# A preactivation chain of four convolution layers on one core: where the U-Net's 5x5 layer, conv2 and conv3 put their outputs

## The chip, the cores and the metric

The kernel runs on one core of a Trainium2 chip. The metric is the device time of one execution in microseconds (us). A core has engines that run side by side, each with its own instruction queue: TensorE (PE, matrix products into PSUM), VectorE (DVE) and ScalarE (ACT, both elementwise), GpSimd (POOL, here only the issue of some table loads) and SyncE (SP, here the issue of nearly all DMA transfers). [...]

## The reference

The input x has 16 samples, 32 channels, 128 x 128 pixels, float32. Four layers follow each other, each with a normalisation in front and a residual sum: a diagonal LSTM (layer 0), an adder layer (layer 1), a layer in the Hartley domain (layer 2) and an edge U-Net (layer 3). Cut to what matters here, layer 3 is:

```python
# five edge operators, each normalised over its sample: 32 -> 160 channels
b = [norm(corr3x3(x, op)) for op in (SOBEL, SCHARR, LAPLACE, ROBERTS, PREWITT)]
y = conv3x3(concat(b), conv1)          # 160 -> 32 channels, 128 x 128
y = maxpool2(y)                         # 64 x 64
y = maxpool2(conv3x3(y, conv2))         # 32 x 32
y = maxpool2(conv3x3(y, conv3))         # 16 x 16
y = conv3x3(y, conv4)                   # 16 x 16
y = conv3x3(deconv2x2(y, deconv1), conv5)   # 32 x 32
y = conv3x3(deconv2x2(y, deconv2), conv6)   # 64 x 64
y = conv3x3(deconv2x2(y, deconv3), conv7)   # 128 x 128
```

Layer 1 is `out[n,f] = -sum |patch - w|` over the 288 values of a 3x3 patch, on quantised values.

## The kernel before

**Stages.** `stage0` does layer 0. Then the samples are taken in four groups of four (`g`, 0 to 3), and 128 partitions hold 4 samples x 32 channels (`blk` is the sample, 32 partitions each). The adder layer (`Differences`) is computed sample by sample and half by half: 72 taps per half (8 blocks of channels x 9), each one instruction of 8192 or 8320 float16 values on ScalarE (L757) or VectorE (L760), summed over channels by TensorE (L647). Layers 2 and 3 (`After`) of a group can begin when its four samples have left the adder layer.

**The order of the work.** A planner, `Weave`, puts the work of `After` for groups 0 to 2 between the taps while the program is built. It keeps planned times of TensorE, VectorE and ScalarE (`weave.pe`, `weave.dve`, `weave.act`), to which the code adds an estimate of each step; each tap goes to the engine that is planned to end it first. `weave.later(us, step)` puts a step off to a planned time, `weave.done(v)` emits it at once, and `yield` hands TensorE time or a pause back to the planner. In this part (the front) `keep_order` fixes the order on every engine as emitted. When the taps are over, `drain` emits the rest of group 2 and the whole of group 3 (`end`, with more buffers) alternately by their planned times; there, the order on the engines is set by the framework's scheduler.

**The first layer of the U-Net.** The five operators and conv1 are one 5x5 convolution, whose weights depend on statistics of the sample: `statistics` (L1401) makes Gram products (L1428) of the frame, VectorE turns them into scales (`es_*`), and `first_layers` folds five tables `v`, loaded through POOL's queue, into the weights `wf` (L1559, L1561). The frame of a group lies in buffers `xp`, a ring of 2 in groups 0 to 2 and of 4 in group 3, each with 20 padded rows of 132 values: a chunk `ch` is 16 rows with two more on each side. `frames` loads the chunks (`load`), normalises them on ScalarE (L1373), stores them padded in DRAM (`store`, `xn`) and, for `conv1`, reads them again from there (`again`, two transfers a chunk).

`conv1` computes chunk by chunk, eight in all. TensorE works in 32 x 32 tiles: for each of 25 taps there are 16 matmuls, one for each sample `blk` and each of four groups of output partitions `j` (L1747). Bank `acc[blk]` then holds sample `blk`; its partitions `32j..` hold the rows 4j to 4j+3 of the chunk, all channels. Before the chunks, `conv1` computes corrections for the left and right border (L1721) into the tile `cut`. Per chunk and bank, VectorE adds two of them to the border columns (L1782), pools 2x2 (`pooled`, L1674) into a 128 x 128 tile, and `spread` adds the bias and writes `y1`. In `y1`, `y2`, `y3` and `y4` the partitions are again sample and channel, `[128, n+2, n+2]` with a border of zeros (`padded`), so the four groups of 32 partitions of a bank go to the same 32 partitions of the target: `spread` takes one instruction for each `j`, four a bank, sixteen a round, on ScalarE for the 5x5 layer and VectorE for conv2 to conv4 (L1685, L1688); in the last phase, when group 3 is alone (`weave.alone`), by halves on both.

```python
for j in range(4):
    d, s = dst(slice(32 * blk, 32 * blk + 32), j), src[32 * j : 32 * j + 32]
```

The emission of a chunk's `spread` is put off by 5 us (`weave.later(5.0, spread)`). That of the last chunk, `rest_of_y1`, is emitted before the second half of conv2.

**The small layers.** `small_layers` runs conv2 (two rounds of 4 x 8 rows), conv3 (one round of 4 x 8 rows), conv4 (one round of 4 x 4), each with 9 taps of 16 matmuls a round (L1597), then the two upsampling layers (L905, L930). `last` does the third upsampling, the residual sum (L1876, L1846) and the output.

Of the kernel before, what the change touches and what calls it, by code (L numbers as in the profile page):

```python
# [492 lines left out]
def rest(nc, tc, cst, sel16, bias, m1, r1, a, d, out):  # L493


    with ExitStack() as ctx:
# [16 lines left out]
        end.buffers = {"t_x": 8, "xm": 8, "xw": 4, "t_w": 6, "t_r": 8, "frames": 4, "gm": 5, "e_v": 6, "l_x": 4}  # L513
# [445 lines left out]
class After:  # L959
# [386 lines left out]
    def frames(self, g, pool):  # L1346
# [5 lines left out]
        ring = [pool.tile([128, 20, W + 4], F32, name=f"xp{i}") for i in range(self.buffers["frames"])]  # L1352
# [4 lines left out]
        chunk = lambda ch: ring[ch % len(ring)]  # L1357

# [35 lines left out]
        def again(ch, half):  # L1394

            own = slice(10 * half, 10 * half + 10)
            nc.sync.dma_start(chunk(ch)[:, own, :], padded(ch, own.start, own.stop))

        return load, normalise, store, again, chunk

    def statistics(self, g, pool, frames, sides, out, tables):  # L1401
# [8 lines left out]
        load, normalise, store, again, chunk = frames  # L1410
# [26 lines left out]
        for ch in range(H // 16):  # L1437
# [3 lines left out]
            for l in range(2, 18):  # L1441
# [29 lines left out]
                def following(ch=ch, half=half):  # L1471
                    if ch + ahead < H // 16:
                        load(ch + ahead, half)
                        ready[ch + ahead, half] = normalise(ch + ahead, half, 18.0)
                    else:
                        again(ch + ahead - H // 16, half)
# [56 lines left out]
    def first_layers(self, g, fp, frames, y2):  # L1533
# [32 lines left out]
        with self.pool("e_y1") as y1p:  # L1566
            y1 = self.padded(y1p, 64, "y1")
# [5 lines left out]
    def small_layers(self, cp, rp, y1, y2):  # L1573
# [3 lines left out]
        if not y1:  # L1577
# [3 lines left out]
            y3, y4, y5 = (self.padded(cp, n, f"y{i}") for n, i in ((16, 3), (16, 4), (32, 5)))  # L1581
# [3 lines left out]
        def conv(src, n, name, evict):  # L1585
            rows = min(n // 4, 512 // n)
            for r in range(0, n, 4 * rows):
                acc = [self.acc() for _ in range(4)]
                if r:
                    weave.done(self.rest_of_y1)  # L1590
                for tap in range(9):
                    kh, kw = tap // 3, tap % 3
                    for j in range(4):
                        for blk in range(4):
                            part = slice(32 * blk, 32 * blk + 32)
                            at = r + rows * j + kh
                            nc.tensor.matmul(  # L1597
                                acc[blk][32 * j : 32 * j + 32, : rows * n],
                                wc[name][part, tap, :],
                                src[part, at : at + rows, kw : kw + n],  # L1600
                                start=tap == 0,
                                stop=tap == 8,
                            )
                    yield rows * n / 512 * 1.0 + 0.15
                yield SUMMED
                for blk in range(4):
                    evict(r, rows, acc[blk][:, : rows * n], blk)
                yield -2.0

        def pool_into(dst, n, b):  # L1610
            def evict(r, rows, acc, blk):
                top, half = 1 + r // 2, rows // 2
                self.spread(
                    lambda part, j: dst[part, top + half * j : top + half * j + half, 1 : 1 + n // 2],
                    self.pooled(cp, acc, rows, n),
                    blk,
                    bias[:, b : b + 1],
                    nc.vector,
                )

            return evict

        def flat(r, rows, acc, blk):
            self.spread(
                lambda part, j: y4[part, 1 + r + rows * j : 1 + r + rows * j + rows, 1:17],
# [65 lines left out]
    def conv1(self, g, pool, frames, y1, sides, wf, b1):  # L1691
# [45 lines left out]
        for ch in range(H // R):  # L1737
# [37 lines left out]
            if ch + ahead < H // R:  # L1775
                for half in range(2):
                    again(ch + ahead, half)
# [277 lines left out]
```

## Time and profile before

| what | time |
|---|---|
| median of three runs | 6687.31 us (6674.74 to 6688.99) |
| the profiled execution | 6656.74 us |
| its span, first to last instruction | 6655.0 us |
| layer 0 | to about 685 us |
| first to last tap of the adder layer | 685.5 to 5586.6 us |
| the rest of groups 2 and 3 | to 6655.0 us |

The profile shows one execution. Its page gives busy time by engine, the span in 40 slices, the chain that ended last, and groups of instructions by source line, with the number of instructions, their busy time, the mean of one in ns, and the idle time of the engine just before them with what ended it. `32x128 f32` is partitions by elements. Other views answer by stretches of time, by tile, or instruction by instruction. `issue` is time in which an engine waited for nothing that the profile shows. TensorE takes a float32 matmul as two records.

### The profile page before, as it was taken

The numbers are of one execution on the slowest core, as the hardware profiler recorded it, in microseconds if no ns is written. First come the engines' busy times: TensorE is split into PE (matmuls) and PEld (weight loads), VectorE is DVE, ScalarE is ACT, GpSimd is POOL, SyncE is SP. The second block draws the span as 40 slices with busy tenths as digits, with TensorE's granted clock in tenths as the row PEclk, the third lists the DMA queues.
The fourth block names the chain that finished last, engine by engine and source line by source line (L and its number), as shares of the span: only waits on it lengthen the run. The fifth ranks groups of instructions, "written<-read, shape, count | busy, mean of one in ns | idle before, by whom it ended". The sixth has DMA issues, their size and how long they took to land.

```text
span 6655.0 us, 270517 instructions
## 1 busy us (share of the span) xinstructions
PE 5351.9 (80%) x126760; PEld 2793.3 (42%) x126760; DVE 5541.6 (83%) x6848; ACT 5455.3 (82%) x3201; POOL 66.4 (1%) x67
## 2 busy tenths in 40 slices
PE   3698677787777879998877778999787787986896
PEld 3675333333343433333333443333333443444584
DVE  7898899999999889999999999999999996243222
ACT  3898899999999989999999999999999996111112
POOL 0000000000000000000000000000000000000000
PEclk9999899999989989998999899999989898997897
DMA  7553322211343632211553652231355354345314
GB/s 318 209 190 121 80 58 63 54 40 47 76 135 109 185 106 64 66 43 48 115 144 92 176 157 67 66 78 35 79 137 148 88 168 127 133 155 161 100 32 108
DMA packets 380773, 728.15 MB, mean 109 GB/s; under 512 B 73284, under 2 KB 225348, under 8 KB 368772
## 3 DMA queue, kind: packets, MB, share of 16 engines
q1 hardware_dynamic: 372180, 676.41, 35.4%
q0 software_dynamic: 7040, 33.80, 1.5%
q8 instruction: 992, 16.25, 1.0%
q14 instruction: 129, 1.06, 0.1%
q10 hardware_dynamic: 432, 0.64, 0.0%
HBM read 510.69 MB, written 200.00 MB: 107 GB/s over the span
## 4 chain that ended last, share of the span: by engine, by line
issue 33%; PE 29%; DVE 21%; ACT 13%; DMA 4%; SPq 1%; POOL 0%; DVEq 0%; ACTq 0%; POOLq 0%
DVE d_dve L760 12%; PE acc L1747 11%; ACT d_act L757 8%; PE acc L647 7%; PE pg L223 3%; PE acc L905 3%; ACT gt L237 2%; PE acc L1597 1%; DVE stat L124 1%; DVE y L1685 1%; ACT junk L198 1%; PE acc L1428 1%; DMA v<-fold_d 1%; DMA xm_d<-xm 1%; ACT th L247 1%
## 5 line engine op out<-in xcount | busy, mean ns | idle before, releaser
L757 ACT ACTIVATE d_act<-q,neg 128x8192 f16<-128x8192 f16 (+1 forms) x628 | 4443.9, 7150 | 117.1 <-PE acc L647 95.1
L760 DVE TENSOR_SCALAR d_dve<-q,qw 128x8192 f16<-128x8192 f16 (+1 forms) x1676 | 3865.2, 2362 | 165.1 <-PE acc L647 146.1
L647 PE MATMUL acc<-d_dve,sel 128*32 128x512 f16 x26816 | 1874.2, 403 | 491.2 <-DVE d_dve L760 392.6
L647 PEld LDWEIGHTS <-sel 128*32 128x32 f16 x36864 | 1010.6, 100 | 2118.9 <-issue 1461.4
L1747 PE MATMUL acc<-xp,wf 32*32 32x512 f32 x25600 | 1000.9, 610 | 26.0 <-issue 17.5
L647 PE MATMUL acc<-d_act,sel 128*32 128x512 f16 x10048 | 734.1, 414 | 292.4 <-ACT d_act L757 285.3
L1688 ACT ACTIVATE y<-pooled,b 32x128 f32<-32x128 f32 x464 | 185.5, 400 | 513.1 <-DVE pooled L1674 506.8
L1747 PEld LDWEIGHTS acc<-xp,wf 32*32 32x32 f32 x25600 | 422.7, 104 | 373.1 <-issue 292.5
L677 PE MATMUL acc<-q,zero 128*32 128x512 f16 x6268 | 449.3, 399 | 0.0
L905 PE MATMUL acc<-y,u_conv 32*32 32x256 f32 (+1 forms) x9728 | 339.0, 453 | 88.5 <-issue 66.8
L223 PE MATMUL pg<-h,wb 64*64 64x20 f32 (+15 forms) x8192 | 341.4, 305 | 58.8 <-DVE h L251 33.7
L237 ACT ACTIVATE gt<-pg,bias 128x20 f32<-128x20 f32 (+15 forms) x1024 | 332.3, 384 | 40.1 <-PE pg L223 38.1
L223 PEld LDWEIGHTS pg<-h,wb 64*64 64x64 f32 x8192 | 251.5, 151 | 134.2 <-DVE h L251 81.1
L1428 PE MATMUL acc<-xp 32*64 32x204 f32 (+3 forms) x8576 | 241.1, 343 | 42.0 <-issue 40.2
L677 PEld LDWEIGHTS <-zero 128*32 128x32 f16 x6268 | 189.1, 101 | 172.8 <-issue 36.4
L1876 DVE SCALAR_TENSOR_TENSOR xr<-acc,l_one,xr 128x512 f32<-128x512 f32 x128 | 87.1, 743 | 199.0 <-PE acc L905 131.3
L905 PEld LDWEIGHTS acc<-y,u_conv 32*32 32x32 f32 x9728 | 155.6, 109 | 207.2 <-issue 158.1
L1846 ACT ACTIVATE xr<-xr,l_ms 128x1024 f32<-128x1024 f32 x64 | 68.7, 1145 | 209.7 <-DVE xr L1876 199.6
L1428 PEld LDWEIGHTS acc<-xp 32*64 32x64 f32 (+1 forms) x8576 | 170.2, 134 | 123.2 <-issue 115.4
L1782 DVE TENSOR_TENSOR acc<-acc,cut 128x4 f32<-128x4 f32 x256 | 35.3, 165 | 219.3 <-PE acc L1747 217.0
L223 PE MATMUL pg<-xn,wb 64*64 64x2 f32 (+63 forms) x4096 | 184.0, 290 | 25.9 <-issue 17.0
L1597 PE MATMUL acc<-y,w_conv 32*32 32x512 f32 (+2 forms) x4608 | 161.4, 506 | 46.9 <-DMA w_conv<-in_conv_dram 21.3
(218 smaller groups left out, 3653.4 us busy)
## 6 DMA issues: line engine op xcount, KB each, us to landing
q<-q_d SPq DMA_DIRECT2D x128, 536.2 KB, 10.1
xp<-xn_d SPq DMA_DIRECT2D x64, 660.0 KB, 5.0
xp<-x_d SPq DMA_DIRECT2D x56, 640.0 KB, 5.5
xr<-xn_d SPq DMA_DIRECT2D x64, 528.0 KB, 11.7
x_in<-in_x_dram SPq DMA_DIRECT2D x16, 2048.0 KB, 14.7
xn<-in_xs_dram SPq DMA_DIRECT2D x64, 512.0 KB, 7.0
res<-in_x_dram SPq DMA_DIRECT2D x64, 512.0 KB, 8.8
x_d<-res SPq DMA_DIRECT2D x64, 512.0 KB, 4.9
```

The costliest lines, as they stand in the source:

```text
L223: nc.tensor.matmul(bank[c][q][64 * pair : 64 * pair + 64, :, :width], wb[half, 4 * kind + KIND[q]].rearrange("p b o -> p (b o)"), v[half], ...
L237: nc.scalar.activation(gt[:, q, :, :n], bank[c][q][:, :, :n], AF.Tanh if q == G else AF.Sigmoid, bias=bias[:, KIND[q] : KIND[q] + 1],)
L647: self.nc.tensor.matmul(acc[k][32 * j : 32 * j + 32, :], self.sel16[:, i // 9, :], d[:, row : row + 4, c : c + W], start=first, stop=last,)
L677: self.nc.tensor.matmul(acc[k][32 * j : 32 * j + 32, :], self.zero, q[:, :4, :W], start=False, stop=False)
L757: nc.scalar.activation(dst, src, AF.Relu, bias=self.neg[:, i : i + 1])
L760: nc.vector.tensor_scalar(dst, src, self.qw[:, i : i + 1], 0.0, ALU.subtract, ALU.max)
L905: nc.tensor.matmul(acc[blk][32 * j : 32 * j + 32, o : o + rows * n], t[part, 4 * par + tap, :], src[part, top : top + rows, left : left + ...
L1428: nc.tensor.matmul(gram[blk][j : j + width, at : at + n], xp[part, l, 2 + j : 2 + j + width], xp[part, rows, j : j + width + 4], start=sta ...
L1597: nc.tensor.matmul(acc[blk][32 * j : 32 * j + 32, : rows * n], wc[name][part, tap, :], src[part, at : at + rows, kw : kw + n], start=tap == 0,
L1688: nc.scalar.activation(d, s, AF.Identity, bias=bj)
L1747: nc.tensor.matmul(acc[blk][32 * j : 32 * j + 32, :], tap_of("all", tap)[rows], xp[rows, 4 * j + kh : 4 * j + kh + 4, kw : kw + W], start= ...
L1876: nc.vector.scalar_tensor_tensor(v, acc[blk].rearrange("p (b r w) -> p r w b", b=2, w=64), one[:, blk : blk + 1], v, ALU.add, ALU.mult,)
```

## The change

- **Windows instead of chunks.** For `conv1`, `again` reads in one transfer a window of four times 8 padded rows (128 x 4 x 1056 values): rows 4ch to 4ch+7 of each quarter of the image. The ring's buffers have 32 rows instead of 20; group 3 has 3 of them, not 4. In `statistics`, the first windows are read after the last two chunks. Group of partitions `j` of a bank is now quarter `j` of the image.
- **`y1` and `y3` by quarters.** `quartered` makes tiles `[128, 4, n/4+2, n+2]`: the partitions are quarter and channel, the second dimension is the sample. So a bank of the 5x5 layer or of conv3 goes to the same partitions that it lies in, with one instruction of 128 partitions (`evict`). `neighbours` copies the rows at the boundaries of the quarters between groups of 32 partitions, on VectorE: for `y1` after chunks 0 and 7, for `y3` after conv3.
- **conv2 and conv4** read `y1` and `y3` (matmuls: partitions are a quarter, `j` the sample), so their banks hold a quarter with sample and channel on the partitions, which is the layout of `y2` and `y4`; also one `evict` a bank. conv2 takes the taps of the middle and lower rows first, and the last chunk's `evict` and copies are emitted before its seventh tap.
- **Corrections.** Left and right are added in one instruction a bank instead of two.
- The scratch for POOL's DMA descriptors is 2048, not 4096.

```diff
-        end.buffers = {"t_x": 8, "xm": 8, "xw": 4, "t_w": 6, "t_r": 8, "frames": 4, "gm": 5, "e_v": 6, "l_x": 4}
+        end.buffers = {"t_x": 8, "xm": 8, "xw": 4, "t_w": 6, "t_r": 8, "frames": 3, "gm": 5, "e_v": 6, "l_x": 4}
...
-        ring = [pool.tile([128, 20, W + 4], F32, name=f"xp{i}") for i in range(self.buffers["frames"])]
+        ring = [pool.tile([128, 32, W + 4], F32, name=f"xp{i}") for i in range(self.buffers["frames"])]
...
+        window = lambda ch: ring[(ch + 8) % len(ring)]
...
-        def again(ch, half):
-            own = slice(10 * half, 10 * half + 10)
-            nc.sync.dma_start(chunk(ch)[:, own, :], padded(ch, own.start, own.stop))
+        def again(ch):
+            t = self.d["xn"]
+            rows = bass.AP(
+                t.tensor, t.offset + g * 128 * PADDED + 4 * ch * PW, [[PADDED, 128], [32 * PW, 4], [1, 8 * PW]]
+            )
+            nc.sync.dma_start(window(ch).rearrange("p (q r) w -> p q (r w)", q=4), rows)
...
-                    else:
-                        again(ch + ahead - H // 16, half)
+                    elif half and ch >= 6:
+                        for n in range(ch - 6, ahead if ch == 7 else 1):
+                            again(n)
...
-            y1 = self.padded(y1p, 64, "y1")
+            y1 = self.quartered(y1p, 64, "y1")
...
+        def conv(name, n, rows, pick, evict, taps=range(9), late=None):
+            acc = [self.acc() for _ in range(4)]
+            for i, tap in enumerate(taps):
+                if i == 6 and late:
+                    weave.done(late)
+                for j in range(4):
+                    for blk in range(4):
+                        part = slice(32 * blk, 32 * blk + 32)
+                        nc.tensor.matmul(
+                            acc[blk][32 * j : 32 * j + 32, : rows * n],
+                            wc[name][part, tap, :],
+                            pick(part, blk, j)[:, tap // 3 : tap // 3 + rows, tap % 3 : tap % 3 + n],
+                            start=i == 0,
+                            stop=i == 8,
+                        )
...
-            yield from conv(y1, 64, "conv2", pool_into(y2, 64, 1))
+            for half in range(2):
+                yield from conv(
+                    "conv2",
+                    64,
+                    8,
+                    lambda part, blk, j: y1[part, j, 8 * half :],
+                    lambda blk, acc: self.evict(
+                        y2[:, 1 + 8 * blk + 4 * half : 5 + 8 * blk + 4 * half, 1:33],
+                        self.pooled(cp, acc, 8, 64),
+                        bias[:, 1:2],
+                        blk,
+                    ),
+                    [3, 4, 5, 6, 7, 8, 0, 1, 2],
+                    None if half else self.rest_of_y1,
+                )
...
+    def evict(self, dst, src, b, blk, engine=None):
+        nc, weave = self.nc, self.weave
+        us = src.free_size() / 960 + 0.1
+        if blk % 2 == 0 if weave.alone else engine is not nc.scalar:
+            nc.vector.tensor_scalar(dst, src, b, None, ALU.add)
+            weave.dve += us
+        else:
+            nc.scalar.activation(dst, src, AF.Identity, bias=b)
+            weave.act += us + 0.15
...
+    def neighbours(self, t, n, above=True, below=True):
+        w = t.shape[3]
+        for q in range(3):
+            a, b = t[32 * q : 32 * q + 32], t[32 * q + 32 : 32 * q + 64]
+            if above:
+                self.nc.vector.tensor_copy(b[:, :, 0, 1 : w - 1], a[:, :, n, 1 : w - 1])
+            if below:
+                self.nc.vector.tensor_copy(a[:, :, n + 1, 1 : w - 1], b[:, :, 1, 1 : w - 1])
+        self.weave.dve += 3 * (above + below) * (4 * (w - 2) / 960 + 0.1)
...
-                            xp[rows, 4 * j + kh : 4 * j + kh + 4, kw : kw + W],
+                            xp[rows, 8 * j + kh : 8 * j + kh + 4, kw : kw + W],
...
-                for s, col in enumerate((0, W - 1)):
-                    nc.vector.tensor_tensor(a4[:, :, col], a4[:, :, col], cut[:, blk, s, ch, :], ALU.add)
-                weave.dve += 0.3
+                sides_of = acc[blk].rearrange("p (r w) -> p r w", w=W)[:, :, :: W - 1]
+                both = cut[:, blk, :, 4 * ch : 4 * ch + 4].rearrange("p s r -> p r s")
+                nc.vector.tensor_tensor(sides_of, sides_of, both, ALU.add)
+                weave.dve += 0.17
...
-            def spread(top=1 + R // 2 * ch, out=out):
-                for blk in range(4):
-                    self.spread(
-                        lambda part, j: y1[part, top + 2 * j : top + 2 * j + 2, 1:65],
-                        out[blk],
-                        blk,
-                        b1[:, blk : blk + 1],
-                        nc.scalar,
-                    )
+            def spread(ch=ch, out=out):
+                for blk in range(4):
+                    self.evict(
+                        y1[:, blk, 1 + 2 * ch : 3 + 2 * ch, 1:65], out[blk], b1[:, blk : blk + 1], blk, nc.scalar
+                    )
+                if ch in (0, 7):
+                    self.neighbours(y1, 16, ch == 7, ch == 0)
...
-    nc = bacc.Bacc("TRN2", target_bir_lowering=False, num_devices=1, dynamic_dma_scratch_size=4096)
+    nc = bacc.Bacc("TRN2", target_bir_lowering=False, num_devices=1, dynamic_dma_scratch_size=2048)
```

## The prediction, made before the result was known

> **What bounds the kernel now.** I read the page from the top: the span, then the forty slices.
>
> ```profile
> span 6655.0 us, 270517 instructions
> ...
> PE   3698677787777879998877778999787787986896
> DVE  7898899999999889999999999999999996243222
> ACT  3898899999999989999999999999999996111112
> ```
>
> Up to slice 33 (about 5,590 us) VectorE and ScalarE are full and TensorE is not; from there on it is the reverse. So there are two stages with different limits: the long loop of the adder layer, with groups 0 to 2 of the other layers woven in (I call it the front), and the drain, in which the rest of group 2 and all of group 3 run. The groups by line say what the two full engines do:
>
> ```profile
> L757 ACT ACTIVATE d_act<-q,neg 128x8192 f16<-128x8192 f16 (+1 forms) x628 | 4443.9, 7150 | 117.1 <-PE acc L647 95.1 <-DMA co_c<-in_conv_dram 18.1 <-issue 3.2
> L760 DVE TENSOR_SCALAR d_dve<-q,qw 128x8192 f16<-128x8192 f16 (+1 forms) x1676 | 3865.2, 2362 | 165.1 <-PE acc L647 146.1 <-DMA co_c<-in_conv_dram 16.2
> L1688 ACT ACTIVATE y<-pooled,b 32x128 f32<-32x128 f32 x464 | 185.5, 400 | 513.1 <-DVE pooled L1674 506.8
> L1685 DVE TENSOR_SCALAR y<-pooled,bias 32x128 f32<-32x128 f32 (+1 forms) x168 | 45.3, 269 | 3.6
> L1685 DVE TENSOR_SCALAR y<-acc,bias 32x64 f32<-32x64 f32 x56 | 15.8, 282 | 11.4 <-PE acc L1597 10.5
> L1782 DVE TENSOR_TENSOR acc<-acc,cut 128x4 f32<-128x4 f32 x256 | 35.3, 165 | 219.3 <-PE acc L1747 217.0
> L1561 DVE SCALAR_TENSOR_TENSOR wf<-v,ops,wf 128x1440 f32<-128x1440 f32 (+2 forms) x48 | 55.8, 1213 | 8.1 <-DMA v<-fold_d 8.1
> ```
>
> A tap costs ScalarE 7.15 us and VectorE 2.36 us, and a tap can go to either engine: what one of them no longer has to do becomes taps. Then the busy time by stretch (columns: the stretch, its length, busy us of each engine with its instructions, granted clock, DMA share, GB/s):
>
> ```profile
> 685.00:5590.00 4905.00, 4013.43 (x86874) 1857.21 (x86873) 4663.80 (x3914) 4754.20 (x1164) 56.00 (x45) 0.93 0.35 94
> 5590.00:5635.00 45.00, 38.21 (x978) 21.53 (x982) 10.35 (x46) 3.81 (x2) 0.00 (x0) 0.89 0.78 215
> 5635.00:5977.00 342.00, 316.99 (x8812) 165.59 (x8804) 113.00 (x309) 53.88 (x131) 5.15 (x10) 0.95 0.40 130
> 5977.00:6001.00 24.00, 2.30 (x106) 1.74 (x109) 9.42 (x48) 9.98 (x23) 0.65 (x2) 0.58 0.95 372
> 6130.00:6200.00 70.00, 40.73 (x1672) 28.22 (x1644) 38.74 (x94) 4.29 (x4) 2.14 (x4) 0.62 0.44 117
> 6340.00:6472.00 132.00, 131.88 (x4168) 111.49 (x4163) 24.60 (x89) 14.69 (x37) 0.00 (x0) 1.00 0.05 18
> ```
>
> In the front ScalarE is idle for 151 us of 4905 and VectorE for 241: either sets its length. In the drain TensorE is 93 to 100% busy while there is 5x5 work, and has holes at 5977 and 6130. The timeline shows the first hole:
>
> ```profile
> 5977.49 10.13 SPq L1392 DMA_DIRECT2D xn_d<-xp  x8
> 5987.71 12.81 SPq L342 DMA_DIRECT2D w_conv<-in_conv_dram  x8
> 6000.51 4.56 PE L1597 MATMUL acc<-y,w_conv 32*32 32x256 f32 x128 [21.30 <-DMA w_conv<-in_conv_dram]
> ```
>
> conv3's weights stand behind eight frame stores on SP, and TensorE waits 21.3 us for them.
>
> [...] The trace has 0.58 granted in the hole at 5977 and 1.00 in the full stretch at 6340. [...]
>
> **The change part by part, in the front.** The order in which the built instructions stand gives the counts up to the last tap; the durations are those above.
> - ScalarE: 5x5 evictions 256 to 64. A 32x128 one takes 0.400; the new one is 128x128. [...] the trace's 128x128 ACT copy (L1377) took 0.298. I take 0.400: -192 x 0.400 = -76.8. The plan then gives ScalarE four more taps, 632: +28.6. Sum -48.2.
> - VectorE: four taps fewer, -9.4. conv2 and conv3 evictions 96 to 24: -72 x 0.269 = -19.4. conv4's 32 to 8: -24 x 0.282 = -6.8. Edge corrections 128 to 64, twice the elements at 0.17: -21.1 + 10.9 = -10.2. New boundary copies, 24 of 32x256 or 32x64: [...] no row here shows one. [...]
> - Moved: in the new order the front ends before group 2's statistics tail and its folding of weights (25 small operations, 5 us start to start; 15 `wf` operations, 2.0 + 14.0): -21 on VectorE, owed in the drain. VectorE in all: -61.
> - New waits: the copies after chunks 0 and 7 of the 5x5 layer wait on VectorE for four ScalarE evictions (1.6 us), which may stand behind a tap (7.15), so 0 to 8.8 us for each of four in the front; the taps and TensorE's sums are queued behind. The plan places a ScalarE tap to end at most about 3 us behind VectorE, and one VectorE tap mostly stands in between: I take 0.8 each, 3 in all.
> - Memsets, tap order and TensorE's work: nothing. Counts of 3x3 and 5x5 matmuls are unchanged; the 396 more zero matmuls fill slack (TensorE has 890 us of it in the front). If TensorE were late, taps would wait, as they do for 241 us now (146 + 95).
> - Windows: 64 loads of 660 KB become 32 of 2,112 KB, 26 MB more. At the 215 GB/s of the second stretch one takes 10 us, under a 5x5 chunk of 31 us (1000.9/32). Without that cover it would be 10 us a chunk. On SP each stands, as before, behind the end of the chunk that frees its buffer.
> - [...] The last group's six are issued 170 us before use; elsewhere a later issue waits for VectorE anyway. Nothing (0 to +5).
>
> The front thus loses 48 (ScalarE) to 61 us (VectorE): 55, less 3, is **-52**.
>
> **In the drain.** Before, group 2's 5x5 layer begins 7 us after the last tap (5593.4 against 5586.6). Now it waits for the tail (5.1 us), folding (2.0 + 13.6), the adder's last finish (5.6, in between), small operations (2) and waits for tables (about 4, as at 5538 to 5561 now): 33. Then the side corrections, 352 matmuls, 11 us (44.4 busy over four groups). Start at 44, so +37 with TensorE mostly idle. What comes back: in the new order half of conv2 (10.5 us) lies behind group 3's first statistics, and conv3's weights stand behind five stores, not eight; most of the 21.3 us hole should close, -15. The final chain has shorter evictions between conv2, conv3, conv4 and conv5: about -4 (2 ScalarE and 2 VectorE operations for 8 and 8, less six copies). Three frame buffers for four: ten instead of eight statistics halves go through the serial load, normalise, store steps on SP (8.4 us each at 6044 to 6070); 0 to +17, and I take +2, as TensorE has more work beside them. Sum **+20**.
>
> Net -32: 6656.7 (span 6655.0 plus 1.7 around it) becomes 6625. The median of the runs, 6687.3, lies 30.6 above that execution; with the same offset the forecast is **6655**.
>
> **Rivals.**
> 1. The drain pays nothing: the late folding hides beside group 3's transforms and all holes close. -52 and -4 at the end give 6631. For it: 190 us of idle TensorE in the drain (1065 less the busy time of its stretches, 873). Against: at its start nothing else is ready.
> 2. The drain gives back what the front wins: +37, no hole closed, +17 for the third buffer, -4, against -52: 6685. That is also the case in which the change does what it says and moves its gain away.
> 3. Slower, by one mechanism: the displaced group 2. Everything of it starts 37 us later, so 128 matmuls of the last layer (10.5 us) and half of conv2 (10.5) fall into stretches where TensorE is already full (93 to 100%), on top of rival 2, and the front wins only ScalarE's 48 less 3: 37 + 17 + 21 - 4 - 45 = +26, thus 6713. It decides once the drain grows by more than about 65 us. Against it: conv2's half has the hole at 5977.
>
> **How the numbers follow.** Chances: forecast 0.50, rival 1 0.16, rival 2 0.17, rival 3 0.17. Bounds of the unknown costs: waits for ScalarE 0 to 35 us, copies +-2, third buffer 0 to 17, new eviction 0.30 to 0.40 (up to 6 us less). Range 6616 to 6706; the forecast alone, 6635 to 6674. 0.2% is 13 us, about what can be told from no change: faster 0.66, same 0.17, slower 0.17.
>
> **What would show it.** Right: the last tap ends near 5535; evictions 128x128 take 0.40; ScalarE has 632 taps; the first 5x5 matmul of the drain comes some 44 us after the last tap; no 21 us wait for `w_conv`. Wrong: copies that idle VectorE for over 20 us in all; 5x5 matmuls that wait for windows; last tap later than 5560; a drain of over 1,110 us (now 1,068).

## The result, and the profile after

The changed kernel takes 6662.2 us (median of 9 runs) beside 6675.1 us before: ratio 0.9979, 95% interval 0.9968 to 0.9989. That is 13 us or 0.21% less, where 32 were forecast. The first trace of before (6656.7 us) lies below every timed run of that kernel (6659 to 6696 us in all); a second trace, taken during the experiments, is at 6671.7 us. Stages are compared with the second one here. The counts of TensorE's instructions in all views are records, two to a float32 matmul: the 4608 of L1600 below are 2304 matmuls, 4 groups of 4 rounds of 9 x 16.

The page of the changed kernel, first the span and the slices:

```profile
span 6662.1 us, 270540 instructions
...
PE   3698677787777879998777787999877786896796
DVE  7898899999999889998999998999999995144112
ACT  3898899999999989999999998999999992011002
```

The two full engines end earlier: in slice 34 (from 5,496 us) ScalarE is busy 2 tenths where it was 6, and TensorE's stretch alone begins with a dip. The groups by line (columns as before) answer the rows of the prediction:

```profile
L757 ACT ACTIVATE d_act<-q,neg 128x8192 f16<-128x8192 f16 (+1 forms) x632 | 4471.7, 7149 | 110.6 <-PE acc L647 87.5 <-DMA co_c<-in_conv_dram 18.0 <-issue 4.5
L760 DVE TENSOR_SCALAR d_dve<-q,qw 128x8192 f16<-128x8192 f16 (+1 forms) x1672 | 3857.2, 2361 | 196.4 <-PE acc L647 176.4 <-DMA co_c<-in_conv_dram 16.2
L1709 ACT ACTIVATE y<-pooled,b 128x128 f32<-128x128 f32 x118 | 43.5, 398 | 511.5 <-DVE pooled L1684 511.3
L1824 DVE TENSOR_TENSOR acc<-acc,cut 128x8 f32<-128x8 f32 x128 | 18.5, 166 | 209.5 <-PE acc L1790 209.4
L1729 DVE COPY y<-y 32x256 f32<-32x256 f32 (+1 forms) x24 | 5.7, 238 | 6.1 <-ACT y L1709 5.6
L1731 DVE COPY y<-y 32x256 f32<-32x256 f32 (+1 forms) x24 | 5.7, 236 | 3.7 <-ACT y L1709 3.1
L1600 PE MATMUL acc<-y,w_conv 32*32 32x512 f32 (+2 forms) x4608 | 144.0, 478 | 30.0 <-issue 24.1 <-DVE pooled L1684 3.9 <-PE acc L1600 1.0
```

Every price of the front holds: 632 ScalarE taps, 0.398 us for the new eviction, 0.166 for the joint edge correction, 0.24 in the mean for a boundary copy (0.29 for 32x256, 0.19 for 32x64). The 21.3 us wait of conv3 for `w_conv` is no longer among L1600's releasers. L760's row waits 176 us for TensorE's sums; in the two traces of before it was 146 and 152.

The busy time by stretch says where the rest went. The stretches end at the last tap, at the first 5x5 matmul of the drain, at the end of group 2's 5x5 layer, at the end of group 3's statistics, at its first and its last 5x5 matmul, and at the end (columns: stretch, length, busy us of TensorE, its weight loads, VectorE, ScalarE, GpSimd with their instructions, granted clock, DMA share, GB/s). Before, second trace:

```profile
685.00:5597.40 4912.40, 4012.34 (x86814) 1853.67 (x86816) 4661.44 (x3911) 4754.46 (x1164) 54.62 (x45) 0.93 0.35 94
5597.40:5605.40 8.00, 2.49 (x65) 0.98 (x60) 5.32 (x11) 0.00 (x0) 0.00 (x0) 0.88 0.39 100
5605.40:5953.80 348.40, 322.54 (x9176) 168.11 (x9176) 98.13 (x272) 48.61 (x114) 0.00 (x0) 0.97 0.45 139
5953.80:6141.00 187.20, 131.84 (x3951) 79.87 (x3949) 66.01 (x221) 45.08 (x82) 5.83 (x11) 0.81 0.61 182
6141.00:6213.10 72.10, 43.04 (x1716) 29.79 (x1708) 40.36 (x100) 4.29 (x4) 2.14 (x4) 0.62 0.44 116
6213.10:6486.10 273.00, 258.91 (x8381) 195.32 (x8392) 48.26 (x146) 41.70 (x84) 0.00 (x0) 0.98 0.21 55
6486.10:6669.90 183.80, 122.01 (x4386) 85.51 (x4374) 59.85 (x140) 47.53 (x80) 0.00 (x0) 0.78 0.46 104
```

After:

```profile
685.00:5543.50 4858.50, 3969.81 (x86542) 1848.33 (x86542) 4602.34 (x3727) 4699.77 (x976) 46.84 (x38) 0.94 0.36 97
5543.50:5605.00 61.50, 11.97 (x734) 9.77 (x733) 31.47 (x87) 3.81 (x2) 3.75 (x7) 0.54 0.78 242
5605.00:5953.70 348.70, 316.67 (x9205) 172.52 (x9204) 98.72 (x232) 11.31 (x28) 2.67 (x5) 0.95 0.42 137
5953.70:6110.30 156.60, 124.69 (x3904) 70.47 (x3904) 41.69 (x151) 37.75 (x67) 3.15 (x6) 0.84 0.51 168
6110.30:6184.30 74.00, 35.16 (x1422) 23.54 (x1424) 41.51 (x105) 6.95 (x8) 2.16 (x4) 0.60 0.55 141
6184.30:6481.80 297.50, 268.93 (x8685) 194.11 (x8661) 39.47 (x92) 20.95 (x32) 0.00 (x0) 0.96 0.29 80
6481.80:6662.10 180.30, 115.52 (x4388) 76.56 (x4380) 52.74 (x115) 36.41 (x50) 0.00 (x0) 0.77 0.47 106
```

Line by line the lengths differ by -53.9, +53.5, +0.3, -30.6, +1.9, +24.5 and -3.5. The front wins 54; the drain grows by 46 (1072.5 to 1118.6). Two stretches carry the loss: the start of the drain, in which TensorE is busy 12 of 61.5 us, and group 3's 5x5 layer. That makes -8 from trace to trace, and -13 by the medians.

The start of the drain, the main steps of TensorE's timeline after the change (start, length, what, and in brackets the idle time ahead of it and what ended it):

```profile
5543.55 1.05 PE L647 MATMUL acc<-d_dve,sel 128*32 128x512 f16 x16 [0.66 <-DVE d_dve L760]
5569.44 0.56 PE L786 MATMUL acc<-ns_mean,cw 128*128 128x4 f32 x2 [24.84 <-DVE ns_mean L783]
...
5579.93 0.29 PE L1748 MATMUL acc<-cw,wf 128*32 128x4 f32 x8 [6.87 <-DVE wf L1566]
...
5588.15 0.96 PE L1764 MATMUL acc<-sides,wf 32*32 32x32 f32 x71 [4.72 <-issue]
...
5595.73 1.53 PE L1764 MATMUL acc<-sides,wf 32*32 32x32 f32 x128 [6.06 <-issue]
5599.48 1.53 PE L1764 MATMUL acc<-sides,wf 32*32 32x32 f32 x128 [2.22 <-issue]
...
5605.04 2.01 PE L1790 MATMUL acc<-xp,wf 32*32 32x512 f32 x32
```

The folding ends 36 us after the last tap (33 were forecast). But the side corrections (L1764) then take 25 us where 11 were forecast: 15 us of it are idle stretches (holes, for short) with no releaser, `issue`. Which transfers run meanwhile, SP's timeline shows:

```profile
5551.56 4.86 SPq L340 DMA_DIRECT2D x_d<-xr  x8
5556.92 34.49 SPq L1052 DMA_DIRECT2D xh<-x_d  x8
5591.77 4.55 SPq L342 DMA_DIRECT2D w_conv<-in_conv_dram  x4
```

Group 3's first transforms load their eight `xh` blocks exactly then (the last lands at 5598.9). In the second trace of before, these loads were issued from 5605 on, beside the 5x5 layer.

What are the holes? The page's third part has a queue of instructions:

```profile
q8 instruction: 995, 16.30, 1.0%
```

It moves packets of 16,384 bytes. I set them against TensorE's holes of over 1.4 us without a releaser in the drain. Before (first trace) there are 28 of them, after 45; in 26 and in 43 of them such a packet ends 1.1 to 1.8 us ahead of the hole's end (median about 1.45 after). That is no chance: only some 14% of the drain lies so far behind a packet's end, and of the eight equally long holes that have a releaser none does. In the drain after, TensorE has 56,611 records of matmuls and weight loads, and 222 such packets end: one for 255 records. Most of the long holes stand 256 records, or a multiple of that, apart (36 of the 44 distances to within 4). So I take it that TensorE had no instructions then; no view shows the fetch itself. All its holes without a releaser in the drain sum to 118 us before and 164 after.

In the front one loss stands out that no step of the prediction had. TensorE in group 1:

```profile
3999.13 1.95 PE L647 MATMUL acc<-d_act,sel 128*32 128x512 f16 x16
4019.33 0.29 PE L1748 MATMUL acc<-cw,wf 128*32 128x4 f32 x8 [18.25 <-DVE wf L1566]
```

and ScalarE at the same place:

```profile
4034.03 14.24 ACT L757 ACTIVATE d_act<-q,neg 128x8192 f16<-128x8192 f16 x2 [23.13 <-PE acc L647]
```

The plan put the bias matmul of group 1 two pairs of taps' sums after the statistics' last matmul (four to five pairs before the change). The folding wasn't done, TensorE waited 18 us, and the taps' sums stood behind it.

### The profile page after: what moved, and what is told of

Read it like the earlier page. It is cut to its first block, busy times and chain, and to the rows that moved or that the text cites. A ratio compares the mean times of both kernels' runs of the same rounds, so it can differ in the third digit from the quotient of the medians.

```text
span 6662.1 us, 270540 instructions
## 1 busy us (share of the span) xinstructions
PE 5308.8 (80%) x127156; PEld 2771.7 (42%) x127156; DVE 5469.8 (82%) x6556; ACT 5331.0 (80%) x2835; POOL 61.0 (1%) x67
## 4 chain that ended last, share of the span: by engine, by line
issue 34%; PE 30%; DVE 19%; ACT 14%; DMA 3%; SPq 1%; POOL 0%; DVEq 0%; ACTq 0%; POOLq 0%
DVE d_dve L760 11%; PE acc L1790 11%; ACT d_act L757 10%; PE acc L647 8%; PE pg L223 3%; PE acc L905 3%; ACT gt L237 2%; PE acc L1600 2%; PE acc L1432 1%; ACT junk L198 1%; DVE stat L124 1%; DVE y L1695 1%; DMA v<-fold_d 1%; ACT th L247 1%; PE acc L1764 1%
## 5 line engine op out<-in xcount | busy, mean ns | idle before, releaser
L760 DVE TENSOR_SCALAR d_dve<-q,qw 128x8192 f16<-128x8192 f16 (+1 forms) x1672 | 3857.2, 2361 | 196.4 <-PE acc L647 176.4
L677 PE MATMUL acc<-q,zero 128*32 128x512 f16 x6664 | 475.8, 397 | 0.2 <-issue 0.2
L1709 ACT ACTIVATE y<-pooled,b 128x128 f32<-128x128 f32 x118 | 43.5, 398 | 511.5 <-DVE pooled L1684 511.3
L1824 DVE TENSOR_TENSOR acc<-acc,cut 128x8 f32<-128x8 f32 x128 | 18.5, 166 | 209.5 <-PE acc L1790 209.4
L1374 ACT ACTIVATE xp<-xp,shift,stats 128x1280 f32<-128x1280 f32 (+1 forms) x64 | 91.4, 1432 | 121.6 <-DMA xp<-x_d 83.7
```

What stands on the lines that cost most here:

```text
L677: self.nc.tensor.matmul(acc[k][32 * j : 32 * j + 32, :], self.zero, q[:, :4, :W], start=False, stop=False)
L760: nc.vector.tensor_scalar(dst, src, self.qw[:, i : i + 1], 0.0, ALU.subtract, ALU.max)
L1374: nc.scalar.activation(v, v, AF.Identity, bias=self.shift3, scale=self.stats3[:, 1])
```

## The experiments

Three causes for the missing gain stood against each other: TensorE waits for instructions behind the larger transfers; the third buffer and the displaced group 2 cost more than forecast; the front is held back at the place just shown. In the table, the last tap, the time from it to the first 5x5 matmul and the length of the drain are from the trace of each kernel; the median and the ratio are from its timed runs, the ratio to runs of the kernel before that were timed beside them. Where the intervals of two kernels overlap, the difference between them is not clear of the noise.

| kernel | last tap | to first 5x5 | drain | median | ratio, 95% interval |
|---|---|---|---|---|---|
| before, second trace | 5597.4 | 8.0 | 1072.5 | 6675.1 | 1 |
| after | 5543.5 | 61.5 | 1118.6 | 6662.2 | 0.9979, 0.9968 to 0.9989 |
| third_buffer_right | 5597.0 | 8.5 | 1088.7 | 6687.1 | 1.0012, 1.0005 to 1.0018 |
| quarter_windows_2 | 5547.7 | 62.0 | 1100.3 | 6645.3 | 0.9952, 0.9939 to 0.9965 |
| small_first_loads | 5537.2 | 54.6 | 1123.3 | 6656.1 | 0.9969, 0.9958 to 0.9979 |
| evict_by_four_2 | 5578.6 | 18.1 | 1091.8 | 6671.0 | 0.9989, 0.9980 to 0.9997 |
| merged_same_plan | 5571.7 | 16.4 | 1084.0 | 6657.5 | 0.9972, 0.9961 to 0.9983 |
| before_with_hold | 5559.7 | 54.3 | 1109.5 | 6671.2 | 0.9991, 0.9983 to 0.9999 |
| hold_corrections_2 | 5511.3 | 42.7 | 1093.4 | 6634.3 | 0.9937, 0.9923 to 0.9951 |
| hold_half_windows | 5524.2 | 49.1 | 1092.6 | 6624.8 | 0.9921, 0.9908 to 0.9933 |

**The third buffer alone.** The kernel before with three frame buffers in group 3:

```diff
-        end.buffers = {"t_x": 8, "xm": 8, "xw": 4, "t_w": 6, "t_r": 8, "frames": 4, "gm": 5, "e_v": 6, "l_x": 4}
+        end.buffers = {"t_x": 8, "xm": 8, "xw": 4, "t_w": 6, "t_r": 8, "frames": 3, "gm": 5, "e_v": 6, "l_x": 4}
```

> The kernel before with three frame buffers (of 20 rows) in group 3 instead of four; the order of everything up to the last tap stays as it is. My step: +2 us in the drain (0 to +17), in group 3's statistics, so 6675 becomes 6677. Rival: the smaller ring alone costs 10 us or more and is what the drain gave back. Besides, the front is the same instruction for instruction: if its last tap ends within 3 us of 5586.6 the traces' fronts can be compared to that accuracy, if 10 us away they cannot.

It took 6688.6 us against 6679.4 (ratio 1.0013, 1.0006 to 1.0019). But with three buffers the re-read of chunk 0 lands in the buffer that still waits for chunk 6, so group 3's statistics there are of other rows. The next run puts the re-reads into the right buffers, and `conv1` takes them from there:

```diff
-            nc.sync.dma_start(chunk(ch)[:, own, :], padded(ch, own.start, own.stop))
+            nc.sync.dma_start(ring[(ch + 8) % len(ring)][:, own, :], padded(ch, own.start, own.stop))
...
```

> The kernel before with three frame buffers in group 3, and the first re-read chunks placed in the buffers that the 5x5 layer takes them from (in the run before this one the re-read of chunk 0 went over chunk 6). Everything up to the last tap is the same, so this is also a second trace of the front before. My step: +2 us (0 to +17), 6679 becomes 6681. Rival: 10 us or more, 6689 or later, with group 3's statistics stage (188.7 us from the end of group 2's 5x5 layer in the trace of before) 10 us longer.

Ratio 1.0012, some 8 us (3 to 12 by the interval), with the stretch up to the end of group 3's statistics at 201.8 us (187.2 in the second trace of before):

```profile
5955.10:6156.90 201.80, 148.25 (x4301) 83.48 (x4296) 68.17 (x225) 45.49 (x82) 5.82 (x11) 0.81 0.56 166
```

TensorE is busy 16 us longer in this stretch than in before's, with 350 more records, so it is not shown that the serial loads of the forecast's step are what makes it longer. The step's direction and bounds hold, its value of +2 does not. This is the price in the kernel before; in the changed kernel it wasn't tried.

**A second trace of before.** 

> The kernel before, unchanged, for a second trace. Two runs with its instruction order up to the last tap ended that tap at 5598.8 and 5597.0, not at 5586.6. If the first trace was at the low edge of what this kernel does, the last tap is near 5597 and the drain near 1079 (the median 6678 less 5597 and 1.8 around the span); if not, near 5587 and 1068.

The last tap ended at 5597.4 and the drain took 1072.5 us: the first trace was at the low edge, by 11 us in the front alone. Four traces share before's order up to the last tap (5586.6, 5598.8, 5597.0, 5597.4) and three share the changed kernel's (5543.5, 5547.7, 5537.2). Their means are 5594.9 and 5542.8: the change takes 52 us from the front.

**Fewer bytes in the windows.** In groups 2 and 3 only the first quarter is loaded (GpSimd also sets rows 20 to 31 of their buffers to zero, in lines left out here):

```diff
...
-            nc.sync.dma_start(window(ch).rearrange("p (q r) w -> p q (r w)", q=4), rows)
+            to = window(ch).rearrange("p (q r) w -> p q (r w)", q=4)
+            if g >= 2:
+                to, rows = to[:, :1], bass.AP(t.tensor, rows.offset, [[PADDED, 128], [32 * PW, 1], [1, 8 * PW]])
+            nc.sync.dma_start(to, rows)
```

> The changed kernel in which the window loads of groups 2 and 3 read one of the four quarters (528 KB for 2,112), so three quarters of the 5x5 layer's input are stale there; the order of instructions stays. Theory fetch: TensorE's holes without a releaser in the drain (163.6 us after, 118.5 before) are waits for its own instructions behind the window loads; they shrink by 25 to 40 us, the first 5x5 matmul of the drain comes about 48 us after the last tap instead of 61.5, group 3's 5x5 stage takes about 285 instead of 297.5, and the time falls by some 30 us to 6632. Rival order: the drain is longer only because the work stands in another order; the holes stay within 5 us and the time within 5 us of 6662.

6645.3 us, some 17 less than the changed kernel (25 to 40 were expected of the holes, 30 of the time). Holes without a releaser fell from 164 to 144 us. The two 5x5 stretches shrank, the others did not (the same windows as before, for this kernel):

```profile
5547.70:5609.80 62.10, 12.16 (x740) 9.87 (x739) 31.56 (x88) 3.81 (x2) 3.73 (x7) 0.52 0.77 239
5609.80:5946.30 336.50, 316.59 (x9205) 174.56 (x9204) 98.63 (x232) 11.31 (x28) 6.78 (x8) 0.96 0.37 113
...
6178.40:6466.70 288.30, 267.45 (x8686) 199.77 (x8661) 39.57 (x93) 20.95 (x32) 0.00 (x0) 0.96 0.23 55
```

348.7 became 336.5 and 297.5 became 288.3, with TensorE's busy time unchanged within 1.5 us: what went are holes. So bytes that lie under 31 us of matmuls, which the prediction put at nothing, cost time in this kernel: 20 us of holes in the drain, which I take to be waits for instructions. This is not yet the price of the change: the run takes 1,584 KB off each load, and the change had added only 792 (a chunk's two loads were 1,320 KB before). In proportion to those 17 us the added bytes would cost some 8, an estimate that no run tests. The start of the drain stayed at 62 us: there the windows are not the cause.

**Fewer bytes in the first loads of group 3.**

```diff
-                    nc.sync.dma_start(xh, bass.AP(x2.tensor, first, [[W, H], [HW, 16], [1, W]]))
+                    n_c = 4 if g == 3 else 16
+                    nc.sync.dma_start(xh[:, :n_c], bass.AP(x2.tensor, first, [[W, H], [HW, n_c], [1, W]]))
...
```

> The changed kernel in which the eight loads of xh for group 3 read 4 of 16 channels, which its first transforms then use four times over (group 3's transforms are of other data). The run with quarter windows left the start of the drain at 62.0 us with the same 15 us of holes, so the window loads are not its cause; the eight xh loads lie there instead, from 5557 to 5599. Theory: the tables for the folding and TensorE's instruction fetches wait behind them; with a quarter of the bytes the first 5x5 matmul comes 45 us after the last tap for 61.5, the side corrections take 13 us for 25, and the time falls by 10 to 16 us to about 6650. Rival: 704 small matmuls at half the clock cannot go faster than one fetch at a time; the start stays within 5 us of 61.5 and the time within 5 us of 6662.

The start shrank from 61.5 to 54.6 us and the corrections from 25 to 19. The time is some 6 us less, but the intervals overlap, and the drain as a whole is not shorter in this trace (1123.3 us). The holes in the corrections became equal:

```profile
5578.50 0.96 PE L1765 MATMUL acc<-sides,wf 32*32 32x32 f32 x71 [2.34 <-issue]
...
5582.24 1.53 PE L1765 MATMUL acc<-sides,wf 32*32 32x32 f32 x128 [2.22 <-issue]
5585.99 1.53 PE L1765 MATMUL acc<-sides,wf 32*32 32x32 f32 x128 [2.22 <-issue]
5589.73 0.63 PE L1765 MATMUL acc<-sides,wf 32*32 32x32 f32 x38 [2.21 <-issue]
```

The DMA engines were idle by then. Beside each other, in the columns of the stretches above, a hole of the changed kernel and 4 us of this run (a packet counts where it starts, so a share can pass 1):

```profile
5589.67:5595.73 6.06, 0.00 (x1) 0.00 (x0) 0.00 (x0) 0.00 (x0) 0.00 (x0) 0.50 1.05 293
5582.00:5586.00 4.00, 1.54 (x131) 1.41 (x131) 0.00 (x0) 0.00 (x0) 0.00 (x0) 0.50 0.02 4
```

So both theories have their share. Beside full queues (DMA share 1.05) a hole is 4.7 to 6.1 us; with the queues free (0.02) it is 2.2, and 128 records of these small matmuls (64 matmuls) with their weight loads take 3.75 us, of which TensorE works 1.53. The forecast's 11 us, from busy time, were out of reach here: with the queues free, the 704 records (352 matmuls) took about 19. The granted clock is 0.50 in both; what a higher clock would change was not tried.

**Four evictions for one**, with the new layout kept:

```diff
                 for blk in range(4):
-                    self.evict(
-                        y1[:, blk, 1 + 2 * ch : 3 + 2 * ch, 1:65], out[blk], b1[:, blk : blk + 1], blk, nc.scalar
-                    )
+                    for j in range(4):
+                        p = slice(32 * j, 32 * j + 32)
+                        self.evict(
+                            y1[p, blk, 1 + 2 * ch : 3 + 2 * ch, 1:65], out[blk][p], b1[p, blk : blk + 1], blk, nc.scalar
+                        )
```

> The changed kernel with each 128-partition eviction of the 5x5 layer issued as four of 32 partitions, as before the change, the layout kept. Theory: the evictions are the 77 us that ScalarE got free, and they are worth it because a tap can go to either engine; ScalarE does 628 taps or fewer again, the last tap comes 25 to 45 us later than 5543.5 and the time rises by 20 to 40 us to about 6690. Rival: TensorE's sums bound the front, and the evictions are worth less than 10 us.

The front moved as expected: 626 ScalarE taps, last tap at 5578.6, 31 to 41 us later than in the three traces of the changed kernel. The time did not: about 7 us longer (ratios 0.9989 and 0.9979), and the intervals overlap. In the longer front the plan had finished group 2's folding and 192 of the 704 records of its side corrections, and the 5x5 layer began 18.1 us after the last tap:

```profile
685.00:5578.60 4893.60, 4004.07 (x86486) 1858.70 (x86489) 4636.50 (x3777) 4739.37 (x1162) 50.10 (x45) 0.93 0.36 97
5578.60:5596.70 18.10, 9.03 (x560) 6.54 (x559) 5.37 (x11) 3.81 (x2) 0.00 (x0) 0.69 0.65 178
```

**One eviction, planned as four.** Up to the last tap, the order on ScalarE and VectorE is that of the run before this one, with a single instruction for each four:

```diff
             def spread(ch=ch, out=out):
                 for blk in range(4):
+                    if blk % 2 == 0 if weave.alone else False:
+                        weave.dve += 3 * (128 / 960 + 0.1)
+                    else:
+                        weave.act += 3 * (128 / 960 + 0.25)
```

> The changed kernel, planned as if each eviction of the 5x5 layer still cost four instructions: the order on the engines is that of evict_by_four_2, with one instruction in place of four. Theory: ScalarE has 77 us less to do in the front, but no tap moves over, so VectorE, which has the same work as there, sets the end: 10 to 25 us faster than 6671, say 6653. Rival: ScalarE alone sets the pace, and most of the 77 us come out: 6620 or less. Second rival: what counts is the plan's places, not the engines' load: within 5 us of 6671.

6657.5 us: the instructions alone, at one order, are worth some 11 us (0.9972 beside 0.9989; the intervals overlap by a little, so the size is uncertain). ScalarE's waits for TensorE's sums rose from 99 to 167 us, so most of the 77 us became idle time, as no tap moved over. And this kernel isn't slower than the changed one (0.9972 beside 0.9979), though its front ends 28 us later: its drain is 35 us shorter, so in these traces the drain pays what the front wins by letting taps move over.

**A pause ahead of the corrections**, in the front only:

```diff
                 if len(v) < 10:
                     table()
                 yield -1.2
+            if not weave.draining:
+                yield -12.0
```

> The changed kernel with a planned pause of 12 us (in the front only) between the folding of a group's weights and its first bias matmul, so that 5 instead of 2 pairs of taps' sums stand ahead of it in group 1. Theory place: 23 us of ScalarE and 8 us of VectorE in the front were lost at 4019 to 4049 because TensorE waited there 18.3 us for the folding with sums queued behind; without it the last tap comes 10 to 20 us earlier, at about 5528, and the time falls by about 10 us, less what group 2's later start costs the drain. Rival bound: TensorE is the front's third bound, the waits move elsewhere, and the last tap stays within 5 us of 5543.5.

6634.3 us, 28 less than the changed kernel, more than expected. The wait for the folding is gone, but a smaller one stands nearby, for another reason:

```profile
3988.25 4.03 PE L647 MATMUL acc<-d_act,sel 128*32 128x512 f16 x32 [17.22 <-DVE xr L628]
```

ScalarE waits 14.9 us there instead of 23.1. The front is 19 to 32 us shorter (5511.3 here, 5524.2 with the same order in the last run below; this trace, at 6606.4 us, lies 28 under the kernel's median, so its stages show more than the runs gain). VectorE's waits for TensorE in the front fell from 211 us to 175 and 185, in several places, ScalarE's stayed (109 to 107 and 117). The drain is 25 us shorter; seven of the eight `xh` loads now stand behind `w_conv` on SP, so the folding and its tables no longer meet them. That the named place is the whole cause is refuted; how the 28 us divide among these is not settled.

**The same pause in the kernel before.** 

> The kernel before with the same planned pause of 12 us ahead of a group's first bias matmul (7, 7 and 1 pairs of taps' sums in between, for 5, 4 and 3). Theory place: before, no such stall was there to remove (the bias matmul of group 1 waited under 1 us), so the pause gains nothing or costs what the later start of group 2 costs: 6679 within 8 us, or slower. Rival: the pause makes a better plan whatever the layout, and before gains some 20 us or more as the changed kernel did, 6655; then the 28 us are no part of what the change lost.

6671.2 us, ratio 0.9991. The front became 38 us shorter, the drain 37 us longer:

```profile
685.00:5559.70 4874.70, 3999.42 (x86566) 1852.16 (x86566) 4651.30 (x3896) 4743.88 (x1163) 49.70 (x40) 0.93 0.35 93
5559.70:5614.00 54.30, 12.88 (x740) 9.91 (x741) 24.66 (x59) 3.81 (x2) 2.95 (x6) 0.50 0.88 273
```

The pause gains some 6 us here, within the 8 that the theory allowed, so most of the 28 us are won in the changed kernel alone. And this is the displacement by itself, without the change's new layout: part of group 2's folding and all of its corrections leave the front, it ends earlier, and TensorE idles for the same work at the start of the drain. Hardly anything is won. The later stretches, too, do what they did in the changed kernel:

```profile
5614.00:5967.30 353.30, 315.63 (x9204) 173.40 (x9203) 99.53 (x254) 44.82 (x112) 2.66 (x5) 0.94 0.40 126
5967.30:6117.90 150.60, 113.14 (x3716) 68.50 (x3718) 51.93 (x195) 39.22 (x74) 3.16 (x6) 0.86 0.51 165
...
6186.40:6481.30 294.90, 272.85 (x8833) 203.91 (x8835) 51.17 (x145) 49.22 (x96) 0.00 (x0) 0.97 0.26 65
```

From the second trace of before, the stretch up to the end of group 3's statistics shrinks by 36.6 us, with no wait of conv3 for `w_conv` left, and group 3's 5x5 stretch grows by 21.9. The holes without a releaser in the drain are 161 us (118 before, 164 after the change), with the old frame loads. So the larger windows are not needed for more holes, nor the new layout of conv2 for closing the `w_conv` hole.

**Both together.** With the pause, and in the drain every window after the first loading four new rows a quarter, the other four copied from the window before it:

```diff
...
+            t, top = self.d["xn"], 0
+            to = window(ch).rearrange("p (q r) w -> p q (r w)", q=4)
+            if ch and weave.draining:
+                old = window(ch - 1).rearrange("p (q r) w -> p q (r w)", q=4)
+                nc.scalar.copy(to[:, :, : 4 * PW], old[:, :, 4 * PW :])
+                top = 4
...
```

> The changed kernel with the pause, and in the drain each window but the first loads only its four new rows a quarter (1,056 KB for 2,112); the other four are copied on ScalarE from the window before it. Theory fetch: TensorE's instruction fetches wait behind fewer bytes; a quarter of the bytes gave 17 us, half gives 6 to 12: 6634 becomes about 6626. Rival: the copies (about 2.4 us each on ScalarE, behind the chunk that frees the buffer) put the window later and eat it: no change within 4 us, with 5x5 matmuls waiting for ScalarE.

6624.8 us, ratio 0.9921: the fastest of all, some 11 us under the run with the pause alone; with four and seven runs and intervals that overlap, that is not clear of the noise. The thirteen copies took 1.96 us each on an idle ScalarE; the expectation's 2.4 was the author's estimate.

## Why the prediction came out as it did

- **The front, -52: right.** The traces give -52 in the mean. Its terms too: evictions -77.1 on ScalarE, four taps +28.1 (both against the first trace); VectorE's busy time fell by 59.1 (61 forecast, net of 6 for the 24 boundary copies, which was the author's estimate; at the 0.24 us measured they come to 5.8).
- **Waits of the copies, 3 (0 to 35): small.** 7.3 us in the front, and under the 20 us that would have told against it. In the longest, 3.4 us up to 3,049.4 us, VectorE ran nothing until ScalarE's eviction had ended, then three copies and four taps without another wait. So the taps behind stood still with it, as the step supposed, but in all it cost little.
- **An unforeseen stall in group 1** took 23 us of ScalarE's and 8 of VectorE's time; the -52 is what remained. That the sum still came out is luck: by the stretches above ScalarE is idle for 158 us of the front before and 159 after, so other waits became shorter by as much, and no term had that either. The stall is no property of the layout: it came with the places in the plan, where four to five pairs of sums became two (evict_by_four_2, in the same layout, has three, and TensorE waits 1.8 us there).
- **The drain, +20: this step failed.** It grew by 46. By its terms:
  - Start of the 5x5 layer at 44: it was 61.5. Folding 36 for 33. The term that was mis-sized is the 11 us of corrections, 25 measured: busy time left out the holes (19 us in all with the queues free), and beside the `xh` loads a hole was 4.7 to 6.1 us instead of 2.2.
  - `w_conv`'s hole, -15: the stretch up to the end of the statistics shrank by 30.6. The wait went entirely, more than forecast. The reason given is there (conv3's weights stand behind five stores, and half of conv2 runs while they travel), but it isn't needed: before_with_hold, in the old layout, closes the hole too.
  - Final chain, -4: -3.5.
  - Third buffer, +2: some 8 us when tried alone in the kernel before.
  - Windows, nothing: wrong in its reason, as bytes under matmuls did cost time. Taking three quarters of them away in groups 2 and 3 gained 17 us, and 20 us of holes went; the bytes taken away are twice those that the change had added, whose own price was not measured.
  - The smaller scratch, nothing (that step is about POOL's six table loads for the last group): not shown, as no run had it alone.
  - Group 3's 5x5 stretch, +24.5: the forecast had no term for it. It holds 14 us more holes and 10 us more of TensorE's work, some 290 more records (145 matmuls) of the last layer than either trace of before: work displaced into a full TensorE, as rival 3 described (128 matmuls were priced there at 10.5 us). before_with_hold has +21.9 of it with the old layout and loads.
- **Which case it was.** Between the forecast and rival 2, in which the drain returns everything: 46 of the 54 us came back from trace to trace. The mechanism of rival 2 was right in kind, the displaced start, and before_with_hold shows it alone: 38 us won in the front, 37 returned. The granted clock was 0.54 in the start of the drain, with TensorE busy 12 of 61.5 us, and 0.95 in the stretch after it, with 317 of 348.7.
- **The total** is nearer than its parts. The forecast of 6655 set off from the median of three runs, 6687; nine runs give 6675, and from there the same -32 would be 6643, with the result 19 above it.

## What to carry to other kernels

Two stages with different bounds trade with each other: cheaper work in the first moves its end ahead of what used to finish under it, and the second begins with that tail on the path (38 us won and 37 returned, with the pause in the kernel before); price the new start of the second stage by what it must wait for, the transfers of others included. A transfer that "hides under matmuls" was not free here: with three quarters of such bytes taken away the kernel was 17 us faster. Instructions come by DMA too, in the drain here one packet of 16,384 bytes for 255 of TensorE's records, so where many short matmuls run, count the bytes that move beside them. Where a planner orders the work, compare at one order, as the run planned as four did, before crediting a gain to an instruction.

## What the runs showed of the hardware

TensorE's holes go with packets of the instruction queue: in the drain of the changed kernel, in 43 of 45 holes of over 1.4 us without a releaser, a 16,384-byte packet ended 1.1 to 1.8 us ahead of the hole's end, and 222 of them came for 56,611 records of matmuls and weight loads. 128 records of matmuls of 32x32 by 32 columns with their weight loads take 3.75 us, 1.53 of it busy, with the DMA engines free (share 0.02, granted clock 0.50); the holes among them, 2.2 us there, are 4.7 to 6.1 us with the engines full (share 1.05). An eviction of 128 x 128 values takes ScalarE 0.398 us and one of 32 x 128 takes 0.400. And the same instruction order ended the front at 5586.6 to 5598.8 us from one execution to the next, another at 5511.3 and 5524.2, so one trace settles no difference under about 13 us.
